# Sending the expert results of early tiles later: half a tile per tile during the routing, the rest behind it

## The chip, the cores and the metric

The kernel runs on one core of one Trainium2 chip. The metric is the device time of one execution in microseconds (us); several runs are taken and their median is compared. A core has a matrix engine (PE, TensorE), a vector engine (DVE, VectorE), a scalar engine (ACT, ScalarE), a general engine (POOL, GpSimd) and a sync engine (SP), which mostly issues transfers. Each engine works through its own list of instructions in order, and semaphores make one engine wait for another.

## The reference

One pre-norm decoder layer on 64 sequences of 128 tokens with 128 features, all float32: self-attention with 16 heads, cross-attention onto a context of 77 tokens, and a mixture of 8 experts of which each token uses 2.

```python
x = x + self_attention(layernorm(x))
x = x + cross_attention(layernorm(x), ctx, mask)
# the mixture of experts, on xn = layernorm(x):
pn = l2norm(xn @ Wp.T)
gate_scores = pn @ l2norm(sim_matrix).T / temperature
top_v, top_i = top_k(gate_scores, 2)
p = softmax(top_v)
h = gelu(xn @ W1[e] + b1[e])          # for the experts e in top_i, 512 wide
x = x + sum over the two experts of p * (h @ W2[e] + b2[e])
```

## The kernel before, in words

**Groups.** The 64 sequences form 16 groups of 4. One long loop, `attention`, runs the self-attention of all groups and then the cross-attention of all groups, a sequence at a time. When a group is done with its cross-attention, `route` normalises its tokens, projects them (L353), finds the two largest gates, counts how many rows each expert has so far, and places each token's row. `scatter` (L449 to L462) then sends the rows, each with its destination and its gate weight, to the table `rows.x` in DRAM: an indirect DMA that POOL issues (L454), eight for each group, kept in the list `sending` until the loop takes them out. Each of them is made to wait for the newest activation of the experts (`behind`), so that it isn't issued ahead of it.

**Tiles.** `experts` is a generator that works on 71 tiles of 256 rows, each of one expert. The first 37 tiles (`rows.early`) hold rows of the groups that were routed first; the rest are called late, since their rows include those of the groups routed last. In iteration t it issues, in this order: for tile t+1 the transposition of its rows on PE (L1131), its copy xT on DVE (L1133), and the cast of the destinations to integers, `at` (L1135, ten buffers); for tile t the first matrix product ph (L1143) on PE and the Gelu hT (L1150) on ACT; for tile t-1 the second product py (L1161) on PE, and bias and gate weight on DVE (L1167, L1170), which leave the result `yr` in one of eight buffers; for tile t+3 the load of its rows on SP (L1117) and the copy of its expert's weights on DVE (L1125).

**Results.** At the end of `output(t-1)` POOL sends the two halves of the result, 128 rows each, to the table `rows.y` in DRAM: for each half a small memset of a tile named `gap` (L1174) and an indirect DMA (L1175) that reads `yr` and `at`. The sends of these rows and the loads behind them are declared free of dependence on one another where the rows can't meet.

**Order.** The order of each engine's instructions is written by hand: the program issues them in the order of the Python code. The loop over the experts (from L1270) does the following after each iteration, as long as t is at most 34 (`rows.early - AHEAD`, AHEAD being 3): two steps `rest()` of what remains of attention and routing, one scatter out of `sending`, and one clearing of table rows. From t = 52 on (`rows.half` is 51) it also gathers the results of the groups whose tiles have all been sent (L1211 on SP), and adds them to x (`combine`, L1226). The results of the last groups are gathered after the last tile.

Of the kernel before, what the change touches and what calls it, by code (L numbers as in the profile page):

```python
# [25 lines left out]
LATER = (6, 7, 8, 11, 12, 13, 15)  # L26
NORM = 2
SPLIT_2 = 14
AHEAD = 3
WARM = (28, 8, 2)  # L30
SPLIT = 11
# [3 lines left out]
def decoder_layer(  # L35
# [18 lines left out]
    E, _, F = w1.shape  # L54
# [60 lines left out]
    for w, n in ((bq, "bq_s"), (bk, "bk_s")):  # L115
        t = W[n] = const.tile([P, 1], F32, tag=n, name=n)
# [160 lines left out]
    class Rows:  # L277
        def __init__(self):
# [3 lines left out]
            self.half = 2 * SPLIT * T // TILE + E - 1  # L282
            self.more = 2 * SPLIT_2 * T // TILE + E - 1
            self.tiles = 2 * n // TILE + E - 1
# [18 lines left out]
    rows = Rows()  # L303
# [25 lines left out]
    def route(g):  # L329
# [7 lines left out]
        def tiny(name, shape=(P, GB, E)):  # L337
            return hp.tile(list(shape), F32, tag=name, name=name)
# [53 lines left out]
        def count():  # L392
# [11 lines left out]
            for b in range(1, GB):  # L404
                nc.vector.tensor_tensor(
                    ahead[:, b, :], ahead[:, b - 1, :], both[:, b - 1, :], ALU.add
                )
            rows.seen = tiny(f"seen{g}" if g in (SPLIT - 1, SPLIT_2 - 1) else "seen", (P, E))
            nc.vector.tensor_tensor(
# [60 lines left out]
    def table(late):  # L470
# [14 lines left out]
        def counts(name, seen):  # L485
            pn = ps_m.tile([P, E], F32, tag="mm", name="pn")
            nc.tensor.matmul(pn, ones_f, seen, start=True, stop=True)
            nc.vector.tensor_copy(tiny(name, (1, E)), pn[:1])
# [12 lines left out]
        def begin():  # L501
# [4 lines left out]
            if late:  # L506
                counts("more", rows.counts[SPLIT_2 - 1])
                counts("every", rows.seen)
# [98 lines left out]
            ]  # L607
        return steps

    newest, sending, clearing, gathered, ready = [None], [], [], [], [0]  # L610
    spots = []

    def apart(inst, group):

        tc.declare_no_dep(inst, group=group, reason="rows of their own")
        tc.add_to_no_dep_group(group, inst)
# [485 lines left out]
    def experts(ff, ps_h, ps_y):  # L1102
        flat = we_s.rearrange("p e w -> p (e w)")
        N = rows.tiles
        V = [dict() for _ in range(N)]

        def fetch(t):
            v = V[t]
            late = t >= rows.early
            n = t - rows.early if late else t  # L1110
            v["x"] = ff.tile([P, 2, DX], F32, tag="x", name="xr", bufs=4)
            v["w"] = ff.tile([P, WE], F32, tag="w", name="wr", bufs=4)
            row = nc.sync.value_load(
                rows.row[late][0:1, n : n + 1], min_val=0,
                max_val=E * rows.step + (E - 2) * TILE,
            )
            i = nc.sync.dma_start(  # L1117
                v["x"], rows.x[bass.ds(row, TILE), :].rearrange("(p h) d -> p h d", p=P)
            )
            if not late:  # L1120
                apart(i.ins, "x late")
            w = nc.vector.value_load(
                rows.wat[late][0:1, n : n + 1], min_val=0, max_val=(E - 1) * WE
            )
            nc.vector.tensor_copy(v["w"], flat[:, bass.ds(w, WE)])  # L1125

        def turn(t):
            v = V[t]
            tp = ps_m.tile([P, TILE], F32, tag="mm", name="tp")
            for h in range(2):  # L1130
                nc.tensor.transpose(tp[:, h * P : (h + 1) * P], v["x"][:, h, 0:D], ident)  # L1131
            v["xT"] = ff.tile([P, TILE], F32, tag="xT", name="xT")
            nc.vector.tensor_copy(v["xT"], tp)  # L1133
            v["at"] = ff.tile([P, 2], I32, tag="at", name="at", bufs=10)
            nc.vector.tensor_copy(v["at"], v["x"][:, :, D])  # L1135

        def hidden(t):
            v = V[t]
            v["h"] = ff.tile([P, NFC, TILE], F32, tag="hT", name="hT")
            for c in range(NFC):  # L1140
                if c % 2 == 0:
                    ph = ps_h.tile([P, 2, TILE], F32, tag="h", name="ph")
                nc.tensor.matmul(  # L1143
                    ph[:, c % 2, :], v["w"][:, c * P : (c + 1) * P], v["xT"],
                    start=True, stop=True,
                )
                if c % 2 == 0:
                    continue
                for n in (c - 1, c):
                    i = nc.scalar.activation(  # L1150
                        v["h"][:, n, :], ph[:, n % 2, :], AF.Gelu,
                        bias=v["w"][:, WF + n : WF + n + 1],
                    )
                    newest[0] = i.ins

        def output(t):
            v = V[t]
            py = ps_y.tile([P, 2, D], F32, tag="y", name="py")
            for h in range(2):
                for c in range(NFC):  # L1160
                    nc.tensor.matmul(  # L1161
                        py[:, h, :], v["h"][:, c, h * P : (h + 1) * P],
                        v["w"][:, F + c * D : F + (c + 1) * D],
                        start=(c == 0), stop=(c == NFC - 1),
                    )
            y = ff.tile([P, 2, D], F32, tag="y", name="yr", bufs=8)
            nc.vector.tensor_tensor(  # L1167
                y, py, v["w"][:, WB : WB + D].unsqueeze(1).to_broadcast([P, 2, D]), ALU.add
            )
            nc.vector.tensor_tensor(  # L1170
                y, y, v["x"][:, :, D + 1 :].to_broadcast([P, 2, D]), ALU.mult
            )
            for h in range(2):
                nc.gpsimd.memset(gap, 0.0)  # L1174
                i = nc.gpsimd.indirect_dma_start(  # L1175
                    out=rows.y,
                    out_offset=bass.IndirectOffsetOnAxis(ap=v["at"][:, h : h + 1], axis=0),
                    in_=y[:, h, :], in_offset=None,
                    bounds_check=2 * B * S - 1, oob_is_err=False,
                )  # L1180
                apart(i.ins, "y")

                rows.results.append((t, i.ins))
                for past, group in rows.loads:
                    if t >= past:
                        apart(i.ins, group)
            v.clear()

        for t in range(min(AHEAD, N)):
            fetch(t)  # L1190
            yield
        turn(0)
        yield
        for t in range(N + 1):
            if t + 1 < N:
                turn(t + 1)
            if t < N:
                hidden(t)
            if t > 0:
                output(t - 1)  # L1200
                ready[0] = t
            if t + AHEAD < N:
                fetch(t + AHEAD)
            yield

    def gather(g, b):

        r = spots.pop(0)
        spots.append(r)
        at = (g * GB + b) * 2 * S  # L1210
        i = nc.sync.dma_start(  # L1211
            r, rows.y[at : at + 4 * S, :].rearrange("(b t k) d -> t b k d", k=2, t=S)
        )
        if g < SPLIT_2:
            past, group = rows.half if g < SPLIT else rows.more, f"y{g} {b}"
            rows.loads.append((past, group))
            for t, o in rows.results:
                if t >= past:
                    tc.add_to_no_dep_group(group, o)
            apart(i.ins, group)  # L1220
        gathered.append((g, b, r))

    def combine():
        g, b, r = gathered.pop(0)
        for k in range(2):
            nc.vector.tensor_tensor(  # L1226
                xs[g][:, b : b + 2, :], xs[g][:, b : b + 2, :], r[:, :, k, :], ALU.add
            )
        if g >= SPLIT_2:
            nc.scalar.dma_start(  # L1230
# [13 lines left out]
    with tc.manual_schedule(  # L1244
# [7 lines left out]
        def beside(n):  # L1252

            if n == 0:
                pools.append(ctx.enter_context(
                    tc.tile_pool(name="ff", bufs=3, reuse_waits="tile")
                ))
                for name, bufs in (("ps_h", 2), ("ps_y", 1)):
                    pools.append(ctx.enter_context(tc.tile_pool(
                        name=name, bufs=bufs, space=bass.MemoryType.PSUM, reuse_waits="tile"  # L1260
                    )))
                first.append(experts(*pools))
            if n < 4 or n > 4:
                next(first[0])

        rest = attention(beside)

        done = [(g, b) for g in range(SPLIT_2) for b in range(0, GB, 2)]
        total, steps = len(done), rows.tiles - rows.half
        for _ in first[0]:  # L1270
            t = ready[0]
            if t <= rows.early - AHEAD:
                for _ in range(2):
# [3 lines left out]
                if clearing:  # L1277
                    clearing.pop(0)()
            if t == rows.early - AHEAD - 1:

# [11 lines left out]
        for g, b in done:  # L1292
            gather(g, b)
# [61 lines left out]
```

## Time and profile before

| | |
|---|---|
| three runs | 1139.87, 1147.22 and 1158.19 us, median 1147.22 |
| the profiled execution | 1138.82 us, of which 1137.1 us is the profile's span |
| PE busy | 1052.5 us, 93% of the span |
| DVE, ACT, POOL busy | 754.6, 607.4 and 520.4 us |
| mean granted clock of PE | 0.931 of full speed |
| scatters of rows to `rows.x` (L454) | 128, 999 ns of POOL each |
| sends of results to `rows.y` (L1175) | 142, 1030 ns of POOL each |
| chain that ended last | PE 81%, DVE 7%, DMA 4% of the span |

A row of the profile's groups names the line, the engine and the operation, what is written and read, how many there were, the busy time and the mean of one, and then how long the engine stood idle just before such instructions and what ended most of that idle time. "issue" means that the profile shows nothing that the engine waited for. The lines of tenths show 40 equal slices of the span; the clock is that which the chip granted to PE. The busy time of POOL for a send is the time in which it prepares the transfer, not the transfer itself.

### The profile page before, as it was taken

Reading aid. Unit: us, or ns where it says so; the run is one execution under the profiler, and the core shown is the slowest. Engines: PE = TensorE matmul, PEld = TensorE weight load, DVE = VectorE, ACT = ScalarE, POOL = GpSimd, SP = SyncE. Lnnn points to the kernel's source line nnn. Section 1 sums busy time; section 2 is a strip of 40 time slices with the busy share of each in tenths; the row PEclk is TensorE's granted clock in tenths of the full one; section 3 lists DMA queues with packets and bytes.
Section 4 is the critical chain, followed back from the end, with each engine's and each line's share of the span. In section 5 each row is a group of like instructions: output and inputs, shape, how many; then the busy total and the mean of one; then the engine's idle time right before and its main releaser. Section 6 shows DMA issues by size and latency. Waiting matters only on the chain.

```text
span 1137.1 us, 41849 instructions
## 1 busy us (share of the span) xinstructions
PE 1052.5 (93%) x17117; PEld 872.3 (77%) x17117; DVE 754.6 (66%) x2303; ACT 607.4 (53%) x1401; POOL 520.4 (46%) x1087
## 2 busy tenths in 40 slices
PE   9999999999999999899999999999887888999893
PEld 5778787877778887777777777888876777999883
DVE  5788888888876675566666666544534567555775
ACT  5566666666666774566556665334434323444341
POOL 7224232334121134455555555344576556556553
PEclk9999999999999996899999998555988989999997
DMA  3111111111134342233322222010121222222665
GB/s 96 41 52 42 42 52 41 51 42 60 51 103 116 94 108 85 84 92 101 119 84 82 83 80 69 30 40 17 50 62 57 62 69 90 71 74 86 185 185 177
DMA packets 87296, 88.76 MB, mean 78 GB/s; under 512 B 19730, under 2 KB 71712, under 8 KB 87104
## 3 DMA queue, kind: packets, MB, share of 16 engines
q1 hardware_dynamic: 76656, 68.30, 20.8%
q0 software_dynamic: 8640, 16.93, 4.6%
q8 instruction: 135, 2.21, 0.8%
q10 hardware_dynamic: 1808, 0.85, 0.3%
q14 instruction: 57, 0.47, 0.1%
HBM read 43.95 MB, written 26.85 MB: 62 GB/s over the span
## 4 chain that ended last, share of the span: by engine, by line
PE 81%; DVE 7%; DMA 4%; issue 4%; ACT 2%; POOL 1%; SPq 1%; DVEq 0%; ACTq 0%; POOLq 0%
PE ps L826 16%; PE pt L826 13%; PE po L888 12%; PE ph L1143 9%; PE py L1161 8%; PE py L927 3%; PE pq L735 3%; PE pt L837 3%; PE pv L761 3%; PE tp L260 2%; PE pp L353 2%; PE pk L747 1%; DMA qh<-mt 1%; DMA xr<-xr 1%; PE tp L1131 1%
## 5 line engine op out<-in xcount | busy, mean ns | idle before, releaser
L873 ACT ACTIVATE e<-pt 128x512 f32<-128x512 f32 (+1 forms) x512 | 276.4, 590 | 241.2 <-PE pt L837 136.0
L848 DVE TENSOR_REDUCE m<-ps 128x4 f32<-128x512 f32 (+1 forms) x512 | 274.2, 577 | 157.0 <-PE pt L837 65.3
L826 PE MATMUL pt<-qh,kh 32*128 32x128 f32 (+1 forms) x4096 | 347.6, 294 | 8.8 <-ACT e L873 6.5
L826 PEld LDWEIGHTS ps<-kh,qh 31*128 31x128 f32 x4096 | 281.0, 194 | 73.5 <-issue 29.6
L826 PE MATMUL ps<-kh,qh 31*128 31x128 f32 (+1 forms) x4096 | 335.9, 291 | 1.4 <-DVE m L848 0.6
L826 PEld LDWEIGHTS pt<-qh,kh 32*128 32x128 f32 (+1 forms) x4096 | 278.6, 173 | 20.1 <-ACT e L873 14.9
L1150 ACT ACTIVATE hT<-ph,wr 128x256 f32<-128x256 f32 x284 | 117.0, 471 | 168.7 <-issue 134.6
L454 POOL DMA_INDIRECT xr<-x,slot x128 | 127.9, 999 | 171.2 <-issue 47.7
L1175 POOL DMA_INDIRECT yr<-yr,at x142 | 146.2, 1030 | 114.3 <-DVE yr L1170 95.1
L1143 PE MATMUL ph<-xT,wr 128*128 128x256 f32 x568 | 147.0, 405 | 16.3 <-ACT hT L1150 5.9
L888 PE MATMUL po<-e,vm 128*32 128x128 f32 (+1 forms) x4096 | 153.1, 288 | 2.9 <-issue 1.8
L1161 PEld LDWEIGHTS py<-wr,hT 128*128 128x128 f32 x1136 | 141.2, 196 | 8.6 <-DVE yr L1167 3.2
L1161 PE MATMUL py<-wr,hT 128*128 128x128 f32 x1136 | 142.1, 279 | 2.3 <-DVE yr L1167 2.1
L1143 PEld LDWEIGHTS ph<-xT,wr 128*128 128x128 f32 x568 | 109.1, 203 | 33.4 <-issue 12.9
L888 PEld LDWEIGHTS po<-e,vm 128*32 128x32 f32 (+1 forms) x4096 | 111.5, 114 | 22.3 <-issue 9.2
L237 POOL TENSOR_SCALAR var<-stat 128x4 f32<-128x4 f32 x48 | 11.2, 233 | 234.6 <-DVE stat L223 233.6
L1167 DVE TENSOR_TENSOR yr<-py,wr 128x256 f32<-128x256 f32 x71 | 30.0, 423 | 105.0 <-PE py L1161 55.8
L837 PE MATMUL pt<-ident_b,in_by_q 32*77 32x128 bf16 x1024 | 71.1, 232 | 4.3 <-issue 3.8
L247 ACT ACTIVATE xn<-xs,shift,rstd 128x128 f32<-128x128 f32 x128 | 62.4, 492 | 19.0 <-POOL shift L241 19.0
L1125 DVE COPY wr<-we_s 128x1156 f32 x71 | 54.3, 765 | 26.3 <-issue 22.9
L837 PEld LDWEIGHTS <-in_by_q 32*77 32x77 bf16 x1024 | 62.2, 124 | 6.8 <-issue 6.0
L222 DVE BATCH_NORM_STATS2 st<-xs 128x6 f32<-128x128 f32 x192 | 54.5, 284 | 4.2 <-DMA xs<-in_x_dram 2.0
(196 smaller groups left out, 1402.8 us busy)
## 6 DMA issues: line engine op xcount, KB each, us to landing
xr<-xr SPq DMA_DIRECT2D x71, 130.0 KB
qh<-qT SPq DMA_DIRECT2D x32, 256.0 KB
in_by_k<-by_k SPq DMA_DIRECT2D x16, 384.0 KB
in_by_q<-by_q SPq DMA_DIRECT2D x16, 308.0 KB
kh<-kT SPq DMA_DIRECT2D x16, 256.0 KB
out_dram<-xs SPq DMA_DIRECT2D x14, 256.0 KB
qh<-yr SPq DMA_DIRECT2D x12, 256.0 KB
kh<-yr SPq DMA_DIRECT2D x12, 256.0 KB
```

Source lines behind the costliest of these rows:

```text
L222: nc.vector.bn_stats(st, xs[g][:, b, :])
L247: nc.scalar.activation(v["xn"][:, b, 0:D], xs[g][:, b, :], AF.Identity, bias=shift[:, i : i + 1], scale=rstd[:, i : i + 1],)
L454: i = nc.gpsimd.indirect_dma_start(out=rows.x, out_offset=bass.IndirectOffsetOnAxis(ap=slot[:, g * GB + b, k : k + 1], axis=0), in_=v["xn" ...
L826: nc.tensor.matmul(pt[:, r, :], v[still][rows, r, b, :], v[moving][rows, r, b, :], start=not side or r == 0, stop=not side,)
L837: nc.tensor.matmul(pt[:, :, 32 * j : 32 * j + wide], v["in", side][rows, j, b, :], mine.unsqueeze(1).to_broadcast([32, HG, wide]), start=F ...
L848: nc.vector.tensor_reduce(v["m", b // 2][:, b % 2, c, :], v.pop(("ps", b, c)), AX.X, ALU.max, negate=True,)
L873: i = nc.scalar.activation(e[:K], pt[:K], AF.Exp)
L888: nc.tensor.matmul(v["o"][32 * c : 32 * c + 32, b % 2, :, j // 2, :], w[:, at : at + 32], v["e", b, c][:K, j, :].rearrange("p (n q) -> p n ...
L1143: nc.tensor.matmul(ph[:, c % 2, :], v["w"][:, c * P : (c + 1) * P], v["xT"], start=True, stop=True,)
L1150: i = nc.scalar.activation(v["h"][:, n, :], ph[:, n % 2, :], AF.Gelu, bias=v["w"][:, WF + n : WF + n + 1],)
L1161: nc.tensor.matmul(py[:, h, :], v["h"][:, c, h * P : (h + 1) * P], v["w"][:, F + c * D : F + (c + 1) * D], start=(c == 0), stop=(c == NFC ...
L1175: i = nc.gpsimd.indirect_dma_start(out=rows.y, out_offset=bass.IndirectOffsetOnAxis(ap=v["at"][:, h : h + 1], axis=0), in_=y[:, h, :], in_ ...
```

## The change

`output` no longer issues the two sends. It appends them to a list `outgoing`, and the iteration takes sends out of the list's front: while t is at most 34, one if at most 12 halves (two for each of the six tiles of `HELD`) are in the list and two otherwise; after that, three as long as there are any. The buffers stay as they are. A gather asserts that no send which it depends on is still in the list.

```diff
@@ -26,6 +26,7 @@
+HELD = 6
@@ -607,7 +608,7 @@
-    newest, sending, clearing, gathered, ready = [None], [], [], [], [0]
+    newest, sending, clearing, gathered, ready, outgoing = [None], [], [], [], [0], []
@@ -1170,11 +1171,13 @@
-            for h in range(2):
+            at = v["at"]
+
+            def send(h):
                 nc.gpsimd.memset(gap, 0.0)
                 i = nc.gpsimd.indirect_dma_start(
                     out=rows.y,
-                    out_offset=bass.IndirectOffsetOnAxis(ap=v["at"][:, h : h + 1], axis=0),
+                    out_offset=bass.IndirectOffsetOnAxis(ap=at[:, h : h + 1], axis=0),
                     in_=y[:, h, :], in_offset=None,
                     bounds_check=2 * B * S - 1, oob_is_err=False,
                 )
@@ -1184,6 +1187,8 @@
+            outgoing.extend((t, lambda h=h: send(h)) for h in range(2))
             v.clear()
@@ -1199,12 +1204,19 @@
             if t > 0:
                 output(t - 1)
                 ready[0] = t
+
+                busy = t <= rows.early - AHEAD
+                for _ in range((1 if len(outgoing) <= 2 * HELD else 2) if busy else 3):
+                    if outgoing:
+                        outgoing.pop(0)[1]()
             if t + AHEAD < N:
                 fetch(t + AHEAD)
             yield
 
     def gather(g, b):
 
+        past = rows.half if g < SPLIT else rows.more if g < SPLIT_2 else rows.tiles
+        assert all(t >= past for t, _ in outgoing)
```

## The prediction

> **What bounds the kernel now.** I read the page first, then the busy time by stretches, then the waits of the stretch that the change touches, last the scatter's own line. From the page, PE, POOL, granted clock and the groups concerned:
>
> ```profile
> span 1137.1 us, 41849 instructions
> PE 1052.5 (93%) x17117; PEld 872.3 (77%) x17117; DVE 754.6 (66%) x2303; ACT 607.4 (53%) x1401; POOL 520.4 (46%) x1087
> ...
> POOL 7224232334121134455555555344576556556553
> PEclk9999999999999996899999998555988989999997
> ...
> L1150 ACT ACTIVATE hT<-ph,wr 128x256 f32<-128x256 f32 x284 | 117.0, 471 | 168.7 <-issue 134.6
> L454 POOL DMA_INDIRECT xr<-x,slot x128 | 127.9, 999 | 171.2 <-issue 47.7
> L1175 POOL DMA_INDIRECT yr<-yr,at x142 | 146.2, 1030 | 114.3 <-DVE yr L1170 95.1
> ```
>
> PE carries the span; POOL has room on the average. The experts lie in the last 350 us, and there the stretches differ (columns: length, busy us of each engine with instructions, granted clock, DMA share, GB/s):
>
> ```profile
> 797.00:824.00 27.00, 23.78 (x154) 21.83 (x153) 15.75 (x56) 11.68 (x29) 15.91 (x30) 0.94 0.18 52
> 824.00:842.00 18.00, 14.20 (x86) 11.69 (x84) 5.21 (x13) 6.43 (x16) 13.98 (x24) 0.93 0.22 68
> 842.00:862.00 20.00, 16.77 (x101) 15.11 (x100) 11.30 (x40) 9.15 (x21) 15.61 (x28) 0.89 0.22 63
> 862.00:971.00 109.00, 89.52 (x545) 79.13 (x544) 63.06 (x214) 38.35 (x94) 65.15 (x118) 0.92 0.23 69
> 971.00:1056.00 85.00, 84.75 (x583) 79.29 (x582) 45.53 (x113) 37.03 (x90) 49.16 (x89) 1.00 0.28 82
> 1056.00:1120.00 64.00, 57.22 (x395) 52.92 (x393) 45.66 (x118) 24.13 (x59) 38.16 (x64) 1.00 0.61 177
> ```
>
> From 797 to 971 the early tiles run beside the last groups' routing, 33 tiles at 5.4 us (the casts of L1135 start at 795.3 and 973.0, 33 apart), and PE is idle for 3.2 + 3.8 + 3.2 + 19.5 = 29.7 us, by the lengths less the busy times of the first four rows. From 971 to 1056 nothing runs beside, PE is full at full clock, and a tile takes 3.77 us (17 casts between 973.0 and 1037.1). What ends the waits in the early stretch:
>
> ```profile
> ACT hT L1150 <- issue: 50.3, 15, 6.9
> POOL yr L1175 <- DVE yr L1170: 41.5, 21, 4.2
> DVE yr L1167 <- PE py L1161: 39.4, 17, 4.7
> ACT hT L1150 <- PE ph L1143: 30.9, 20, 6.0
> ```
>
> POOL waits for the results; no line names POOL as what another engine waits for, and the scatter's own line lists no one behind "who waited for it". One burst deserves a look, POOL and then ACT (start, duration, idle before):
>
> ```profile
> 834.38 0.98 POOL L1175 DMA_INDIRECT yr<-yr,at  x1 [0.19 <-issue]
> 835.33 0.15 POOL L451 MEMSET gap<- 128x1 f32 x1
> 835.67 0.96 POOL L454 DMA_INDIRECT xr<-x,slot  x1 [0.19 <-issue]
> 836.61 0.13 POOL L1174 MEMSET gap<- 128x1 f32 x1
> 836.93 0.99 POOL L1175 DMA_INDIRECT yr<-yr,at  x1 [0.19 <-issue]
> ```
>
> ```profile
> 836.34 0.84 ACT L1150 ACTIVATE hT<-ph,wr 128x256 f32<-128x256 f32 x2 [6.27 <-issue]
> ```
>
> One scatter occupies POOL for 0.98 + 0.15 + 0.19 = 1.32 us. While POOL sends without a pause, ACT stands for 6.27 us for nothing that the profile names. Whether the sends cause that is the open question of this prediction.
>
> **The change part by part.** Nothing is added or removed: 142 y scatters, their memsets, and the same order on PE, ACT, DVE and SP; on POOL alone the y sends move back past the x sends. Counting the loop: iterations 1 to 11 send one half instead of two; 12 to 34 send two, 5 to 6 tiles late; from 35 on three, until the 11 halves left over are gone, about iteration 46 (968 to 1011 by the casts), before the first gather at 52.
>
> First, iterations 1 to 11 (about 797 to 848): 11 scatters fewer, 11 x 1.32 = 14.5 us of POOL. By the waits view this is worth nothing, since nobody waits for POOL. If the bursts do hold PE, the bound is all of PE's idle time there, 3.2 + 3.8 + 1.0 (6/20 of 842 to 862) = 8.0 us, and the clock lost, 27 x 0.06 + 18 x 0.07 + 6 x 0.11 = 3.5: 11.5 us. Against the high end: PE is idle for 19.5 of 109 us (18%) from 862 to 971, with POOL at 60%, and for 21% from 824 to 842, with POOL at 78%; the density of sends explains 3 points of 18 us, 0.6 us. I take 2 us, nearer to this row.
>
> Second, iterations 12 to 34 keep two y sends a tile. They no longer wait for L1170 (41.5 us of POOL waits in the early stretch), so the x sends and routing steps queued behind them on POOL go earlier. Those x sends end at 956.8, while the first late tile is fetched after 971, so their being early gives nothing; the bounds are half of the 19.5 us of idle PE gained, and the same amount lost if ready sends bunch up into bursts like that at 834. I take 0.
>
> The added wait: the cast of L1135 (ten buffers of `at`) must wait until the send that reads the buffer has landed. Before, that send was some nine iterations old; now the buffer of tile t-9 is read by half 2t-17, which is sent first in iteration t-2. Behind the cast on DVE stand the results of L1167, whose waiter is POOL only, and the next weights' copy L1125 and xT, for which PE waits. POOL's occupation per early tile is 110.7/33 = 3.4 us busy and some 0.6 of gaps, 4.0 of 5.4, so it doesn't fall two iterations behind on the average: 0, bounded by 1 us a tile if it does. The y buffers (8, six held and two moving) have the same age and the same answer.
>
> Third, the drain: three sends take 3 x 1.32 = 3.96 us where a tile takes 3.77, so POOL has no pause from about 971 to 1014. Being late by 0.19 a tile, 2 us in all, it keeps no one waiting. Here a rule of the Trainium skill stands against the trace: SBUF — State Buffer, section "SBUF: two separate sides", says that a DMA can't be slowed by a compute operation nor the other way round, which makes the drain free. Its box on DVE and GpSimd-issued DMAs speaks against the change: a float32 copy within SBUF locks GpSimd out of writing descriptors. The row agrees in part: the scatter's longest is 1573 ns against a median of 983 (mean 1030), the copy L1125 takes 765 ns once a tile. By the rule every drain tile pays the 0.59, 3.96 + 0.59 = 4.55 us and POOL 8.6 us late after 11 tiles; by the mean row 3.96 + 3 x 0.05 = 4.1 and 3.6 us late. Neither reaches PE. The burst at 834 contradicts "free": at its 21% idle PE, 43 us of drain cost 9 us. The pairs of sends between 971 and 1056 stand beside 0.25 us of idle PE in 85. Between 0 and 9 I take 3: pairs are the nearer neighbours, but they have a pause and the drain has none.
>
> Sum: -2 + 0 + 3 = +1 us. On the profiled execution, 1138.8 us with 1137.1 of span and 1.7 around it, that is 1140; it lies 8.4 under the median of the three runs (1139.9 to 1158.2), so on the median 1148.
>
> **The rivals.** Likeliest: the sends' order hardly reaches PE, 1140 to 1156, chance 0.52. This includes that the change does nothing at all (1147).
>
> Faster: dense sends do stall PE and ACT. Then the 11.5 us of the first 11 iterations and half of 862 to 971's idle time, 9.8, are gained, and the drain beside a full PE gives little back: -21.3, 1126. For it: the 6.27 us for "issue". Against it: 18% of idle PE at 60% POOL, and routing steps of DVE, PE and ACT that wait for each other anyway. Chance 0.18.
>
> Slower: the wait added at L1135. POOL stands at an x send until Gelu L1150 of its iteration is done, two y sends stand behind it, and the cast two iterations later needs the first of these. It decides where POOL is about one tile (5.4 us) late, as it is in a burst of seven sends like that from 828 to 838. DVE then stands with xT and wr behind it, and PE idles and loses clock: 1 us on each of iterations 12 to 34, 23 us, 1170; with the drain at 9 instead of 3, 1176. For it: early iterations of 2.3 to 4 us lie between ones of 7 to 10, so POOL's distance varies. Against it: the mean of 4.0 in 5.4. Chance 0.30.
>
> **How the numbers follow.** 1148 is the likeliest case. Two per cent of 1147.2, 23 us, is about what a measurement can tell from no change. The range takes most of both rivals, 1128 to 1174, and leaves out about 0.08 below and 0.12 above. Of the faster case two thirds pass 1124 with the runs' own spread (0.12); of the slower one two thirds pass 1170 (0.20); 0.68 stays within.
>
> **What would show it.** Right: 797 to 971 within 3 us of 174 for the same tiles, no "DVE at L1135 <- DMA" among the waits, POOL above 95% occupied over eleven tiles after 971 with PE still above 97% and a tile at 3.8 us. The faster rival shows in the "hT <- issue" sum falling from 50.3 by more than 20; the slower one in waits of L1135 or L1167 for a scatter, or in a drain tile over 4.1 us. I would be wrong if the granted clock of the early stretch moves by more than 0.03, which no step above foresees.

## The result

| | before | changed |
|---|---|---|
| median of 20 runs each | 1139.23 us (1118.04 to 1180.24) | 1147.05 us (1130.47 to 1199.82) |
| ratio | | 1.0148, 95% interval 1.0102 to 1.0194 |
| span of the profiled execution | 1137.1 us | 1143.2 us |

The change makes the kernel slower by about one and a half per cent. The ratio leaves out the slower executions of each kernel (those over 1.5% above its fastest), which is why it isn't the ratio of the two medians; the means of the rest are 1126.2 and 1142.8 us. The time fell into the predicted range and almost on the predicted value of 1148, but by luck: the three runs known then had a median 8 us above that of the twenty. Forecast was +1 us; measured were +8 by the medians and +17 by the ratio.

Busy time by stretches of the changed kernel, the same stretches and columns as before (length, PE, PEld, DVE, ACT, POOL, granted clock, DMA share, GB/s):

```profile
797.00:824.00 27.00, 24.05 (x170) 22.51 (x170) 16.18 (x59) 13.61 (x33) 13.59 (x27) 1.00 0.16 47
824.00:842.00 18.00, 17.24 (x119) 15.77 (x119) 9.11 (x24) 9.88 (x28) 11.17 (x20) 1.00 0.23 68
842.00:862.00 20.00, 14.99 (x101) 13.23 (x100) 11.90 (x45) 8.19 (x17) 13.63 (x22) 0.98 0.21 64
862.00:971.00 109.00, 79.87 (x463) 71.28 (x463) 55.27 (x191) 32.37 (x79) 71.63 (x125) 0.85 0.21 65
971.00:1056.00 85.00, 84.16 (x580) 78.78 (x579) 44.71 (x111) 37.30 (x91) 49.17 (x89) 1.00 0.25 74
```

From 824 to 842 PE was busy for 14.20 us and now is for 17.24, at full clock: the stall that the kernel before had there is gone. From 862 to 971 it fell from 89.52 to 79.87 us, and the clock from 0.92 to 0.85: a larger loss, in a stretch for which the prediction had taken none. From 971 on, where it had put the drain, nothing changed, and POOL is busy for the same 49 us: there is no drain there.

Waits of the changed kernel from 797 to 971 (us in all, times, longest):

```profile
ACT hT L1151 <- issue: 42.9, 12, 12.2
...
DVE yr L1168 <- remote: 19.8, 2, 11.1
...
POOL yr L1178 <- DVE yr L1171: 8.4, 3, 3.4
```

POOL's waits for results fell from 41.5 to 8.4 us, since its sends are old by then. New are two waits of DVE, 11.1 and 8.7 us long, and one of ACT of 12.2. The long ones belong together. POOL's timeline there (start, duration, idle before):

```profile
949.21 1.00 POOL L1178 DMA_INDIRECT yr<-yr,at  x1 [0.19 <-issue]
950.17 0.15 POOL L1177 MEMSET gap<- 128x1 f32 x1
950.51 0.98 POOL L1178 DMA_INDIRECT yr<-yr,at  x1 [0.19 <-issue]
...
962.11 0.98 POOL L1178 DMA_INDIRECT yr<-yr,at  x1 [0.19 <-issue]
963.06 0.14 POOL L1177 MEMSET gap<- 128x1 f32 x1
966.36 0.98 POOL L1178 DMA_INDIRECT yr<-yr,at  x1 [3.16 <-DVE yr L1171]
```

The last x send starts at 947.93. Behind it eleven y sends leave one after the other, 1.29 us apart, without a pause until 963.1: the whole backlog. PE and ACT in that time:

```profile
954.17 1.97 PE L1144 MATMUL ph<-xT,wr 128*128 128x256 f32 x8 [1.19 <-DVE wat L599]
965.68 3.79 PE L1162 MATMUL py<-wr,hT 128*128 128x128 f32 x16 [9.54 <-DVE yr L1168]
```

```profile
965.35 1.57 ACT L1151 ACTIVATE hT<-ph,wr 128x256 f32<-128x256 f32 x4 [12.21 <-issue]
```

The product that hT reads is over at 956.1 by PE's rows, and ACT begins at 965.35, 2.3 us after the end of POOL's last send. PE, with nothing to read, restarts at a granted clock of 0.50 (3.79 us for sixteen products instead of 1.95). A second such stall, 7.2 us of idle PE, lies at 883 to 890, beside eight y sends and four x sends in a row.

The trace also records when each semaphore is updated, and that shows what DVE waited for. Its operation at 965.20 waits for PE's semaphore alone, for none of a transfer. PE's four updates due by then (its rows end at 951.8, 953.0, 955.3 and 956.1) came together, from 965.17 to 965.33. At the second stall none came between 880.19 and 889.59. The 6.27 us of ACT in the kernel before ended with such an update too, at 836.27.

The casts of L1135 (L1136 in the changed kernel), one for each tile, allow the same tiles to be compared whatever happened earlier. In us, from the first cast to the 20th, to the 37th, to the 53rd and to the 70th, with idle PE in brackets:

| kernel | 1 to 20 | 20 to 37 | 37 to 53 | 53 to 70 |
|---|---|---|---|---|
| before | 109.7 (14.1) | 87.5 (15.6) | 60.1 | 71.1 |
| changed | 98.8 (10.8) | 103.8 (27.6) | 60.3 | 70.2 |

In this pair the holding gains 10.9 us, and the stage with the two stalls loses 16.3. One profile of a stage is not exact: in five executions that hold nothing (before, e3, e4, e6, e7) the first two stages took 103.2 to 109.7 and 83.8 to 90.4 us.

### The profile page after: what moved, and what is told of

The parts are those of the page before. It is cut to its first block, busy times and chain, and to the rows that moved or that the text cites. A ratio compares the mean times of both kernels' runs of the same rounds, so it can differ in the third digit from the quotient of the medians.

```text
span 1143.2 us, 41841 instructions
## 1 busy us (share of the span) xinstructions
PE 1051.4 (92%) x17117; PEld 876.0 (77%) x17117; DVE 755.3 (66%) x2303; ACT 607.8 (53%) x1401; POOL 525.0 (46%) x1087
## 4 chain that ended last, share of the span: by engine, by line
PE 82%; DVE 6%; issue 3%; DMA 3%; ACT 2%; another core or an unknown queue 2%; POOL 1%; SPq 1%; DVEq 0%; ACTq 0%; POOLq 0%
PE ps L827 16%; PE pt L827 13%; PE po L889 12%; PE ph L1144 9%; PE py L1162 8%; PE py L928 3%; PE pq L736 3%; PE pv L762 3%; PE pt L838 3%; PE tp L261 2%; PE pk L748 2%; PE pp L354 2%; PE tp L1132 1%; DMA xr<-xr 1%
## 5 line engine op out<-in xcount | busy, mean ns | idle before, releaser
L1144 PE MATMUL ph<-xT,wr 128*128 128x256 f32 x568 | 142.1, 395 | 9.9 <-DVE at L1136 1.7
L1144 PEld LDWEIGHTS ph<-xT,wr 128*128 128x128 f32 x568 | 106.5, 198 | 25.2 <-issue 10.7
```

Source lines behind the costliest of these rows:

```text
L1144: nc.tensor.matmul(ph[:, c % 2, :], v["w"][:, c * P : (c + 1) * P], v["xT"], start=True, stop=True,)
```

## The experiments

Theory A: sends that POOL issues without a pause keep PE's completions from ACT and DVE until the run is over; the changed order makes one long run. Theory B, the slower rival of the prediction in a wider form: the buffers of `yr` and `at` are reused while young sends still read them. The diffs are cut, and are against the changed kernel. The experiments were on three chips: the first four on one; the next six (e5 to e10) on another; the last two on a third. On which chip the two kernels of the result ran isn't on record.

**The run taken away.** e1 paces every y send and spreads the drain.

```diff
                 apart(i.ins, "y")
+                after(i.ins, [newest[0]])
-                for _ in range((1 if len(outgoing) <= 2 * HELD else 2) if busy else 3):
+                for _ in range((1 if len(outgoing) <= 2 * HELD else 2) if busy else 2 + (t % 2)):
```

> The change with each held send made to wait for the newest Gelu activation, as the sends to the x table do, and with the drain at 3 and 2 sends on alternate tiles. Theory A (a run of ready sends on POOL without a pause keeps PE's completions from ACT and DVE until it ends): the two stalls of the changed kernel (PE idle 7.2 us near 881 to 894 and 9.8 us near 954 to 967) are gone or under 2 us each, the 10 us gained in the first 19 tiles stay, ratio to before 0.985 to 0.995. Theory B (the reuse of the y and at buffers waits for sends that are younger than before): the sends are later still, so the stalls stay or grow, ratio 1.01 or more.

Ratio to before 0.9968 (0.9918 to 1.0017), where the change had 1.0148: the loss is gone, but the gain that A expected isn't shown. 1 to 20 take 99.5 us, 20 to 37 take 88.1 instead of 103.8, and the stall near 954 has vanished; at the 20th cast PE is still idle for 6.2 us between 885.5 and 894.3, where A had under 2. The sum of both stages is 9.6 us under that of before, and the whole isn't, as the paced drain now lies where the prediction had put it and costs: 66.3 and 74.8 us from cast 37 to 70, instead of 60.1 and 71.1.

**Less held.** e2:

```diff
-HELD = 6
+HELD = 3
```

> The change with HELD = 3 instead of 6. Theory A: less is held, so the run at the end of the routing has some 7 sends instead of 12 and PE's stall there falls from 9.8 to 3 to 5 us; the early gain falls from 10 to about 5 us; ratio 1.00 to 1.01. Theory B: three more buffers are free, so every wait of L1168 for a send (19.8 us in the changed kernel) is gone, and both stalls with it; ratio 0.985 to 0.995.

Ratio 1.0037 (0.9980 to 1.0095). The last run's stall is down to 3.1 us, as A has it. The stall at the 20th cast stays (7.6 us of idle PE), with three more buffers free: B had both gone. The early gain is lost altogether, 108.1 us for 1 to 20, where A had expected half of it.

**A run where nothing else goes on.** The first attempt, e3, only moved the sends in the program:

```diff
+                for _ in range(0 if 38 <= t < 44 else 14 if t == 44 else 2):
```

> Two sends per tile as before, save in iterations 38 to 43, which hold theirs, and 44, which releases all 14 at once, in the stretch where nothing runs beside the tiles and a tile takes 3.77 us. Theory A: 14 x 1.29 = 18 us of sends without a pause; PE stands for 10 to 15 us within, ACT's hT waits for issue over 10 us although the ph that it reads is done. Theory B: no buffer is reused early enough in the first 2 tiles of the run, so PE loses at most 2 us.

Nothing happened: each tile from the 38th on has its two sends and takes 3.3 to 4.1 us, and PE is idle for 0.3 us from cast 37 to 53. POOL's list has nothing else in this stretch, so that a send written six iterations later is simply issued as soon as its result is there. A place in the program is a place in a queue, and no time. This is what the prediction missed, too.

e6 makes eight halves wait for the Gelu of iteration 41; e7 is the same with six memsets more ahead of each of these sends.

```diff
                 apart(i.ins, "y")
+                if ready[0] == 41:
+                    after(i.ins, [newest[0]])
+                for _ in range(0 if 38 <= t < 41 else 8 if t == 41 else 2):
```

> Two sends per tile as soon as their result is there; the eight halves of the results of iterations 38 to 41 are made to wait for the Gelu activation of iteration 41 and then go as one run of 10.4 us, in the stretch where nothing runs beside the tiles. Theory A: PE idle 5 to 9 us in that run, ACT's hT waits for issue over 5 us, and all goes on within 2.5 us of the last send's end. Theory B (buffer reuse waits for young sends): the next buffer that is still being read is due five tiles later, so PE loses under 1 us.

> The same eight sends, each with six more small memsets ahead of it, about 2.2 us from send to send instead of 1.3. Theory A in its narrow form (a pause of about 1 us lets PE's completions through): PE idle under 2 us over the run, each hT at most 1.5 us late. If it is the number of sends and not their density: 5 us or more, as without the pauses.

The stretch of the run in e6 with its neighbours, then that of e7 (columns as above):

```profile
974.00:996.13 22.13, 22.13 (x156) 20.86 (x155) 12.15 (x31) 9.60 (x24) 9.30 (x16) 1.00 0.21 60
996.13:1015.39 19.26, 13.54 (x80) 11.76 (x79) 6.19 (x16) 4.82 (x13) 11.34 (x21) 0.91 0.18 54
1015.39:1034.00 18.61, 18.61 (x129) 17.26 (x128) 9.87 (x26) 7.84 (x20) 11.11 (x20) 1.00 0.23 71
```

```profile
1013.18:1035.58 22.40, 22.40 (x159) 21.16 (x158) 12.22 (x31) 9.93 (x25) 14.56 (x58) 1.00 0.20 58
```

In e6 three tiles take 19.26 us; in e7 six take 22.40, 3.73 each, with PE never idle. The run of e6 goes from 989.4 to 1005.2, twelve sends: the eight held, and four that came due behind them. Mostly 1.29 us from send to send, it costs 19.26 - 3 x 3.73 = 8.1 us; the eight of e7, 2.7 to 3.2 us apart, cost nothing. But they make POOL late, and what follows in e7 belongs to the picture:

```profile
1034.20:1048.20 14.00, 13.99 (x99) 13.06 (x97) 7.28 (x19) 5.60 (x14) 12.46 (x19) 1.00 0.26 79
1051.40:1074.92 23.52, 15.74 (x98) 13.78 (x97) 8.19 (x22) 5.34 (x15) 18.38 (x32) 0.92 0.28 85
```

Ten sends from 1034.2 to 1048.2, 1.43 us apart on the mean, leave PE busy; fifteen more from 1050.8 to 1070.9, 1.37 apart, leave it idle for 7.8 us. So a run of sends doesn't always stop PE at once; what decides isn't shown.

The waits of e6 in its stretch carry the same signature as those of the changed kernel:

```profile
ACT hT L1151 <- issue: 13.6, 3, 10.2
DVE yr L1168 <- remote: 8.2, 2, 4.7
```

No buffer was due: the tile for which DVE waits 4.7 us reuses the buffer of one that was sent at 970.3, before the holding began. In the changed kernel it was the same: the tile of 965.20 reuses a buffer whose sends left at 936.0 and 939.3. With the semaphores above, that settles B, and it says what "remote" is here: not the landing of a send, but a result of PE that DVE had not been told of.

**POOL busy without sends, and three sends a tile.** e4 has seven memsets behind each pair in iterations 36 to 47; e5 paces all sends, one per tile in 36 to 43 and three in 44 to 51.

```diff
+                if 36 <= t < 48:
+                    for _ in range(7):
+                        nc.gpsimd.memset(gap, 0.0)
```

> Two sends per tile throughout as before; in iterations 36 to 47 seven small memsets follow each pair, so that POOL has hardly a pause, without more transfers. If it is the sends themselves that hold PE (theory A): a tile stays at 3.7 to 4.0 us and PE idle under 1 us over these 12 tiles. If any POOL work without a pause does: PE idle over 5 us. Theory B: no change. All against the same kernel's neighbouring tiles.

```diff
+                after(i.ins, [newest[0]])
+                for _ in range(1 if 36 <= t < 44 else 3 if 44 <= t < 52 else 2):
```

> Every y send waits for the newest Gelu activation; two per tile, one in iterations 36 to 43, three in 44 to 51, where nothing runs beside the tiles. Theory A (sends without a pause hold PE's completions): 36 to 43 stay at 3.7 to 4.0 us a tile without idle PE; 44 to 51, where three sends need 3.9 us, show runs of four and more and lose 5 to 15 us in all. A drain that is only a matter of POOL's time (as the prediction had it): 44 to 51 lose under 3 us.

e4, the twelve tiles with some on either side, and then the moment when POOL, which is late, catches up in a run of twelve sends (1049.2 to 1065.0):

```profile
982.00:1047.00 65.00, 65.00 (x454) 61.26 (x454) 35.06 (x87) 28.12 (x68) 43.93 (x135) 1.00 0.22 65
1052.47:1068.95 16.48, 10.86 (x57) 8.52 (x57) 4.03 (x11) 3.80 (x10) 12.04 (x22) 0.81 0.29 86
```

This work of POOL, seven memsets in 1.1 to 1.7 us between one pair and the next, doesn't disturb PE: not 0.01 us idle in 65. POOL's lateness does, later: two tiles take 16.5 us. e5, eight tiles of one send and seven of three:

```profile
979.34:1009.19 29.85, 29.85 (x211) 28.20 (x210) 16.15 (x42) 13.21 (x33) 10.82 (x20) 1.00 0.21 59
1009.19:1044.89 35.70, 29.68 (x193) 27.35 (x192) 14.37 (x36) 11.79 (x30) 24.03 (x42) 0.94 0.21 63
```

Three a tile make runs of nine and of seven and lose 35.70 - 7 x 3.73 = 9.6 us. This is the price of the drain as the prediction had imagined it, which took 3 between 0 and 9.

**Pauses beside the routing.** e8 holds nothing, and has three more memsets ahead of each send of both tables while the routing goes on.

```diff
+                    for _ in range(3):
+                        nc.gpsimd.memset(gap, 0.0)
                 nc.gpsimd.memset(gap, 0.0)
                 i = nc.gpsimd.indirect_dma_start(
```

> The kernel before with nothing held; each send of either table has three more small memsets ahead of it as long as the routing goes on, about 0.47 us each, 1.8 us from send to send. Theory A: runs without a pause are gone, so the stalls near 830 to 844 go (4 us of PE and the clock), ratio 0.985 to 0.995, as far as 0.5 us is enough of a pause. If POOL's time counts and not the pauses: 3 x 0.47 us on each of 34 tiles, ratio 1.005 to 1.03.

Its four runs took 1169.1 to 1200.9 us beside 1125.4 to 1153.5 for the seven of before, the fastest of each 3.9% apart: worse than either expectation. Its longest waits from 829 to 860:

```profile
ACT e L396 <- DVE e L395: 23.6, 1, 23.6
...
PE ph L1147 <- DVE at L1139: 21.8, 1, 21.8
DVE gate L375 <- POOL gap L453: 20.6, 1, 20.6
```

A different mechanism: the routing has a few operations on POOL (the root that L375 reads), and they stand in the same list behind ten sends, now 2.2 us each. DVE waits for them, PE for DVE, ACT for DVE. In the kernel before, at 1.3 us a send, no wait of L374, the same operation, for POOL is among those from 797 to 971. More is lost behind the routing: the last x send leaves at 991.4 instead of 956.8, PE stands for 21.4 us until the rows of the first late tile have come, and then a run of seventeen sends, 1.36 us apart on the mean, costs PE another 10.3. So pauses can't be had for nothing in this stretch.

**Pacing alone, and the change again.** e9 is the kernel before with each y send waiting for the newest Gelu up to iteration 34, and e10 the changed kernel unaltered.

```diff
+                if ready[0] <= rows.early - AHEAD:
+                    after(i.ins, [newest[0]])
+                for _ in range(2):
```

> Nothing is held: two sends per tile as before, but up to iteration 34 each waits for the newest Gelu activation, as the sends of the x table do; nothing else differs from the kernel before. Theory A: POOL can neither run ahead nor catch up in a run of ready sends. From the first tile's cast to the 37th's some 185 us, as in the paced kernel with three a tile (184.7), where kernels with two unpaced sends needed 187 to 197; from there on as before; ratio 0.985 to 0.995. If the order before was as good: within 0.3% of before.

> The changed kernel once more, beside the one above on the same chip. Theory A: a second profile has the run of ten or more sends where the x sends end, with PE idle over 6 us in it, and 1 to 20 of the tiles some 8 us shorter than in kernels that hold nothing; ratio to before 1.005 to 1.02. If the long stall was an accident of one execution: the run leaves PE idle under 2 us.

e10: ratio 1.014 (1.0049 to 1.0230), with thirteen y sends in a row from 955 to 972 and 11.4 us of idle PE from 955 to 976; 96.8 and 94.5 us for the first two stages. The run behind the x sends and its cost repeat; the stall near the 20th cast doesn't (11.7 us of idle PE from cast 20 to 30, as in the kernel before, against 15.4). e9: ratio 1.0001 (0.9966 to 1.0037), although its stages are short, 101.9 and 84.0 us. The expectation was wrong: the five executions with two unpaced sends reach down to 103.2 and 83.8, and a single profile of these stages doesn't tell a gain of 5 us from the scatter between executions.

**How long a run, how short a pause.** e11 is e7 with two memsets instead of six; e12 is e6 with four held halves.

```diff
+                for _ in range(0 if 40 <= t < 41 else 4 if t == 41 else 2):
```

> The run of eight with two small memsets more ahead of each send, about 1.6 us from send to send: between the run at 1.3, which cost 8 us, and the one at over 2.2, which cost nothing. Theory A: if 0.3 us of pause more is enough, the tiles of the run stay under 4 us on the average; if it takes more, they lose 2 to 8 us as at 1.3.

> A run of four sends without a pause (two tiles' results) instead of eight, in the same place. Theory A: what counts is how long the run lasts beyond the pairs that cost nothing: four last 5.2 us and cost 0 to 3 us, against 8 us for eight.

Neither cost anything: 3.73 us a tile, PE never idle. (The sends of e11 came out 2.0 to 2.6 us apart, not 1.6.) But they don't answer the question, since on the third chip the kernel before took 1065.29 us in its one run, 60 to 80 less than the medians on the others, and there no run of sends in the two profiles does what it did elsewhere. POOL of e12 sends six in a row (its four and the next pair), and ACT's hT starts every 3.73 us as if they were not there. In e11 POOL, late from its eight, sends 23 in a row from 958.2 to 990.5, 1.41 us apart on the mean, and PE is idle for 0.65 us of 33:

```profile
929.88 1.65 ACT L1151 ACTIVATE hT<-ph,wr 128x256 f32<-128x256 f32 x4 [2.08 <-issue]
933.61 1.65 ACT L1151 ACTIVATE hT<-ph,wr 128x256 f32<-128x256 f32 x4 [2.08 <-issue]
```

```profile
958.00:991.00 33.00, 32.35 (x226) 30.10 (x224) 20.13 (x52) 14.36 (x35) 28.37 (x46) 1.00 0.48 144
```

## Why the prediction was right or wrong

**The number was luck.** It came from two terms that were too small and of opposite sign, a drain that isn't there, and a median 8 us too high to start from. Its own signs are divided: no cast waits for a transfer, and the clock from 797 to 971 moved by 0.02; but the tiles between the casts of 795.3 and 973.0 now take 183.3 us instead of 177.7, more than the 3 us allowed, and POOL is busy for 58% of 971 to 1056, not 95%. Two of its chances don't fit each other: 0.12 under 1124 leaves no room for only 0.08 under 1128.

**What bounds the kernel: half right.** PE carries the span, and no line names POOL as what another engine waits for. But "nobody waits for POOL" was read as "POOL's order costs nothing", while the 6.27 us of ACT for "issue" at 836 beside a run of sends, which the prediction showed and called the open question, was the mechanism itself. The semaphores, e1 and e6 show it.

**Iterations 1 to 11: right mechanism, mis-sized.** Taken at -2 between 0 and -11.5; the pair of profiles shows -10.9 from cast 1 to 20, of which 10.0 lie between casts 2 and 13, close to the bound: 3.3 us of idle PE, the rest a busy time shortened by the clock (0.90 from 797 to 880 before, 0.98 now). The sizes within the bound were the other way round, 8.0 of idle time and 3.5 of clock. Over all profiles the gain is less sure: three that hold six tiles (changed, e1, e10) took 96.8 to 99.5 us, 3.7 to 12.9 less than the five that hold nothing. The row that was called nearer, idle PE at 18% from 862 to 971 at a lower share of POOL, was an average over runs and pauses and could not tell the two apart.

**Iterations 12 to 34: the step that failed.** "I take 0", for sends that keep their number and their place. Their place in POOL's list isn't a time. A held send is ready, so what still paced POOL was the x sends' wait for the Gelu; behind the last of them, at 947.9, POOL emptied its list in one run, when PE was at iteration 29 or 30, not 35. The bound "the same amount lost if ready sends bunch up", 9.8 us, had the mechanism, and the measured loss of 20 to 37 is 16.3, of which 12.0 is idle PE and 4.3 a longer busy time at a lower clock (0.85 instead of 0.94 over the stage). In e10 the same stage took 94.5 us.

**The drain: put in the wrong place.** In the change it isn't there: 60.3 us from cast 37 to 53 against 60.1. Where e5 makes it happen, it costs 9.6, at the upper end of 0 to 9. The Trainium skill's rule that a DMA and a compute operation don't slow one another (SBUF — State Buffer, "SBUF: two separate sides") would have made it free; on the two chips where e1 to e10 ran dense sends aren't free, and on the third they were in the 23 of e11. The rule speaks of the ports of that memory, and no run here shows that the delay arises there. Whether the completion of PE or its message is late, the profile can't say either: the ends of matrix products are modelled.

**The added wait at L1135, the slower rival: the wrong cause for the right side.** It priced 23 us and came out on the side that was measured; but no wait of L1136 for a send is in the profile after, and the semaphores, e2 and e6 rule the buffers out.

**Sum.** -10.9 + 16.3 + 0.2 - 0.9 from the first cast to the 70th is +4.7; +2.1 us lies ahead of the first cast, where the code is the same, and -0.7 behind: +6.1 us, the difference of the two spans. The ratio says 17. The pair is not a typical one: the profiled execution of before, 1138.8 us, is 12.7 above the mean of the runs that the ratio compares, that of the change, 1145.1, only 2.3 above its own. That is some 10 of the missing 11 us. In which stage the kernel before lost them isn't shown; the first cast alone lies anywhere between 770.2 and 803.9 us in the profiles of e1 to e10.

## What to carry to other kernels

Moving an instruction back in an in-order list delays it only behind what waits there; if its data is ready and nothing ahead of it waits, it leaves at once, and what was held leaves as a run. To hold work in time, give it something to wait for, and count how many tiles the backlog then needs, with the pauses that the engine beside it wants: here two sends in 3.77 us cost nothing and three cost 1.4 us a tile. And a wait for "issue" of several us that recurs beside one engine's runs is a suspect to price, not noise; the times of the semaphore updates name the engine that was late.

## What the runs showed of the hardware

On two chips, runs of indirect sends from POOL at 1.29 us from one to the next delayed what ACT and DVE learn of PE's finished work: a product over at 951.8 by PE's rows was reported at 965.17. Single reports came through within a run (1001.01 in e6), the rest 1.0 to 2.1 us after its last send ended (both stalls of the changed kernel, e6, e10); PE then started again at a granted clock of 0.50. The same sends 2.7 us or more apart cost nothing (e7), nor did the memsets between pairs (e4). Ten sends 1.43 us apart cost nothing once (e7), so the delay isn't certain. Whether it is POOL's preparing of the sends or the transfers themselves that delay PE isn't separated: no run issues the same transfers from another engine.

On the third chip the delay is nearly absent, also beside the x sends of the attention. In six profiles of the others and of the first pair (before, changed, e3, e6, e9, e10) there are 39 to 50 gaps of over 3 us between PE's semaphore updates after 420 us; in e11 and e12 there are 8. From 450 to 650 us, the kernel before (first pair) and e12 on the third chip:

```profile
450.00:650.00 200.00, 183.62 (x3873) 147.11 (x3869) 127.66 (x495) 117.69 (x298) 105.41 (x218) 0.96 0.32 92
```

```profile
450.00:650.00 200.00, 190.84 (x4556) 158.82 (x4549) 146.23 (x573) 140.31 (x352) 127.28 (x264) 1.00 0.35 104
```

In the same 200 us PE does 4556 products instead of 3873, and e12's edit doesn't touch this stretch. Until the sends begin the two go alike: the first x send starts at 421.6 and at 421.4 us. From there to the first cast they need 358 and 306 us, to the 37th another 197 and 177; from the 37th to the 70th, where only pairs of sends run, 131 and 129. So nearly all that the third chip gains lies where x sends run. What differs between the chips isn't known, and the changed kernel itself was not run on the third: there, by A, it should neither gain nor lose.
